# Moving a norm's centring and row scaling from VectorE to ScalarE, and one weighing past a unit's scores, in a two-layer graph attention kernel

## The chip, the cores and the metric

The kernel runs on one core of a Trainium2 chip. The metric is device time in microseconds (us) of one execution; the figure for the kernel before is the median of 3 runs.

## What is computed

The input x holds 64 graphs of 256 nodes with 512 features, and adj holds a 256x256 mask for each graph. Two attention layers follow one another, all in float32. Cut to what matters:

```
h = max(layernorm(x), 0)                     # layer 0
x = x + attention(h, adj; Wq, Wk, Wv, Wo)    # 4 heads of 64, masked softmax
h = max(layernorm(x), 0)                     # layer 1
h = layernorm(h) * gamma + beta              #   inside the second attention
x = x + attention(h, adj or diagonal; w_qkv, w_out)   # 8 heads of 64
```

In layer 0 the kernel normalises h as (h - mean) * r with r = (var + eps)^-0.5, and takes the maximum with 0 after the transpose. In layer 1 two norms follow each other. Since the first one's scale is positive, max(x - mean, 0) is kept unscaled as h, its own mean and variance are taken, and one row scale r serves both: (h - mean of h) * r.

## The kernel before

The work is cut into 32 steps of two graphs each (T = 512 tokens, four tiles of 128 rows, indexed t = 0 to 3). Each step goes through layer 0 and then layer 1. The heads are handled in pairs ("units"): layer 0 has two, layer 1 has four, written (layer, pair).

For each unit the path is: `project_qk` (L316) makes queries and keys; `scores` (L380) multiplies them, then VectorE adds the mask and takes a row minimum (L399), ScalarE takes the exponential with a row sum (L405), VectorE inverts the sum (L410), and the scaling by it is shared by VectorE (L415, one head of the pair) and ScalarE (L417, the other); `turn` (L420) transposes the result on TensorE, evicted by VectorE (L430) and ScalarE (L432), again one head each; `weigh` (L434) multiplies with the values and ScalarE copies the result out (L450). `combine` (L357) is the output projection, added to the residual by `accumulate` (L286). All projections are done by a fast matrix scheme with seven products on 2x2 blocks, numbered 1, 6, 7, 5, 2, 4, 3 in the order in which they are issued; their blocks need sums, which GpSimd forms (`act_sums`, L94). Products 2, 4 and 3 continue in the PSUM bank of 1, 7 and 5, so product 4 waits for the eviction of 7 (L276), and product 3 for that of 5 (L278).

The norms: `moments` (L196) takes the statistics of a row tile on VectorE (L198, L199). `norm0` (L213) does so for layer 0. `norm1` (L225) takes the statistics of x, centres and clips into h on VectorE (L233), and takes the statistics of h. When the last tile is through, `rsqrt` (L201) lets GpSimd raise the variance to -0.5 (L203), and `scale_row` (L206) subtracts the mean and multiplies by r on VectorE, in place (L208), once for each tile. `transpose_h` (L248) then transposes h on TensorE (L255), and ScalarE (layer 0, L259) or VectorE (layer 1, L261) evicts it.

What sets the order: each call is entered with a period and a place in it by `at` (L463); the calls are sorted by that time and traced in this order. On TensorE the traced order is the queue (L59). On the other engines the planner of the compiler orders instructions by when it expects them to be ready, with the traced order as priority; the result is a fixed queue for each engine. One period of steady work holds layer 1 of step s beside layer 0 of steps s+1 and s+2. Around place 3.0 of a period, TensorE's order is: the last products of `project_qk` for (1,1) and (1,3), `scores` (1,1) at 3.0, `combine` n=1 of layer 0 (entered at 9.0, that is place 3.0 of the period after its own), `weigh` (1,2) at 3.001, two transposes of layer 0, `combine` n=6, two more transposes, and the other products of the combination. Then follow norm1 from place 3.5 on, beside the projection of layer 0's queries and keys, `scores` (1,3) at 3.75, `turn` (1,3) at 4.25 and `weigh` (1,3) at 4.499; the row scaling of that norm is entered at 4.5.

[...] four in the pool "sc" (scores and turns) and four in the pool "mm" (everything else). The tile h has one buffer for both layers.

Of the kernel before, what the change touches and what calls it, by code (L numbers as in the profile page):

```python
# [8 lines left out]
FP = mybir.dt.float32  # L9
U8 = mybir.dt.uint8  # L10
AF = mybir.ActivationFunctionType
ALU = mybir.AluOpType
# [7 lines left out]
def kernel(  # L20
# [16 lines left out]
    nc = tc.nc  # L37
    P = 128
# [5 lines left out]
    NT = G * NIC  # L44
# [11 lines left out]
    stat = ctx.enter_context(tc.tile_pool(name="stat", bufs=4))  # L56
# [13 lines left out]
    mhalf = const.tile([P, NT], FP, name="mhalf")  # L70
# [96 lines left out]
    S = [dict() for _ in range(NSTEP)]  # L167
# [28 lines left out]
    def moments(mv, src, t):  # L196
        bs = stat.tile([P, 6], FP, name="bs")
        nc.vector.bn_stats(bs, src[:, t, :])  # L198
        nc.vector.bn_aggr(mv[:, t, :], bs)  # L199

    def rsqrt(var, name):  # L201
        r = stat.tile([P, NT], FP, name=name, bufs=2)
        nc.gpsimd.tensor_tensor(r, var, mhalf, ALU.pow)  # L203
        return r

    def scale_row(s, t):  # L206
        h, mean, r = S[s]["h"], S[s]["mean"], S[s]["r"]
        nc.vector.tensor_scalar(  # L208
            h[:, t, :], h[:, t, :], mean[:, t, 0:1], r[:, t:t + 1],
            op0=ALU.subtract, op1=ALU.mult,  # L210
        )

    def norm0(s, t):  # L213
        st = S[s]
        if t == 0:
            st["mean"] = stat.tile([P, NT, 2], FP, name="mv0", bufs=2)
        moments(st["mean"], st["h"], t)
        if t == NT - 1:
            ve = stat.tile([P, NT], FP, name="ve0", bufs=2)
            nc.vector.tensor_scalar(ve, st["mean"][:, :, 1], EPS, None, op0=ALU.add)  # L220
            st["r"] = rsqrt(ve, "r0")

    def norm1(s, t):  # L225
        st, x1 = S[s], S[s]["xt"]
        if t == 0:
            st["mv"] = stat.tile([P, NT, 2], FP, name="mv1", bufs=2)
            st["mean"] = stat.tile([P, NT, 2], FP, name="mg", bufs=2)
            st["h"] = act.tile([P, NT, D], FP, name="h")  # L230
        mv, mg, h = st["mv"], st["mean"], st["h"]
        moments(mv, x1, t)
        nc.vector.tensor_scalar(  # L233
            h[:, t, :], x1[:, t, :], mv[:, t, 0:1], 0.0, op0=ALU.subtract, op1=ALU.max
        )
        moments(mg, h, t)
        nc.gpsimd.tensor_tensor(x1[:, t, :], x1[:, t, :], bout_b, ALU.add)
        if t == NT - 1:
            ve = stat.tile([P, NT], FP, name="ve1", bufs=2)
            nc.vector.tensor_scalar(ve, mv[:, :, 1], EPS, EPS, op0=ALU.add, op1=ALU.mult)  # L240
            nc.vector.tensor_tensor(ve, ve, mg[:, :, 1], ALU.add)
            st["r"] = rsqrt(ve, "r1")


    def blocks_of(b, pairs):
# [217 lines left out]
    def at(period, place, fn, *args):  # L463
        events.append((period * PERIOD + place * SET, len(events), fn, args))

    def at_set(period, place, share, fn, *args):
        for i, n in enumerate((1, 6, 7, 5, 2, 4, 3)):
            at(period, place + i * share / 7, fn, *args, n)

    for s in range(NSTEP):  # L470

        p = s - 2
        at(p - 1, 5.6, load_h, s)
        for t in range(NT):
            at(p, 0.4 + 0.4 * t, norm0, s, t)
            at(p, 2.05 + 0.2 * t, scale_row, s, t)
        at(p, 2.9, mask, s, 0)
        for c in range(NC):
            at(p, 3.03 + 0.03 * c, transpose_h, s, 0, c)
        at_set(p, 3.5, 1.0, project_qk, s, 0, 0)  # L480
        at_set(p, 4.5, 0.5, project_v, s, 0)
        at(p, 4.5, scores, s, 0, 0)
        at(p, 5.15, turn, s, 0, 0)
        at(p, 5.6, scores, s, 0, 1)
        at(p, 5.601, weigh, s, 0, 0, True, False)
        at(p, 6.3, turn, s, 0, 1)
        at(p, 7.001, weigh, s, 0, 1, False, True)
        at(p, 7.4, load_x, s)
        at(p, 8.6, first_bias, s)
        at_set(p, 9.0, 0.5, combine, s, 0)  # L490
        for t in range(NT):
            at(p, 9.5 + 0.25 * t, norm1, s, t)
            at(p, 10.5 + 0.1 * t, scale_row, s, t)

        p = s
        for c in range(NC):
            at(p, -0.85 + 0.15 * c, transpose_h, s, 1, c)
        at(p, 0.3, mask, s, 1)
        at_set(p, 0.0, 1.0, project_qk, s, 1, 0)
        at_set(p, 1.0, 1.0, project_v, s, 1)  # L500
        at_set(p, 2.0, 1.0, project_qk, s, 1, 1)
        at(p, 1.0, scores, s, 1, 0)
        at(p, 1.65, turn, s, 1, 0)
        at(p, 2.0, scores, s, 1, 2)
        at(p, 2.001, weigh, s, 1, 0, True, False)
        at(p, 2.65, turn, s, 1, 2)
        at(p, 3.0, scores, s, 1, 1)
        at(p, 3.001, weigh, s, 1, 2, False, False)
        at(p, 3.5, turn, s, 1, 1)
        at(p, 3.75, scores, s, 1, 3)  # L510
        at(p, 3.751, weigh, s, 1, 1, False, False)
        at(p, 4.25, turn, s, 1, 3)
        at(p, 4.499, weigh, s, 1, 3, False, True)
        at_set(p, 5.0, 1.0, combine, s, 1)
        at(p, 6.0, store, s)
# [39 lines left out]
```

## Time and profile before

| | us |
|---|---|
| median of 3 runs | 3907.93 (3907.41 to 3910.31) |
| the profiled execution | 3909.91 |
| its span | 3908.1 |
| TensorE matmul busy | 3641.9 (93%) |
| VectorE busy | 2554.6 (65%) |
| ScalarE busy | 1683.9 (43%) |
| GpSimd busy | 1381.0 (35%) |

In the profile PE is TensorE's matmul, PEld its weight load, DVE is VectorE, ACT is ScalarE and POOL is GpSimd. A group of instructions is named by its line, its engine, and the program's names of its output and inputs (mm<-hT,wqkv). An entry "<- DVE qk L276" says which instruction ended a wait. In a timeline a row has a start, a duration, the engine, the line, the operation and a count; a bracket at its end is the idle time ahead of it. The granted TensorE clock was 0.986 of full speed over the span.

### The profile page before, as it was taken

Reading aid. Unit: us, or ns where it says so; the run is one execution under the profiler, and the core shown is the slowest. Engines: PE = TensorE matmul, PEld = TensorE weight load, DVE = VectorE, ACT = ScalarE, POOL = GpSimd, SP = SyncE. Lnnn points to the kernel's source line nnn. Section 1 sums busy time; section 2 is a strip of 40 time slices with the busy share of each in tenths; the row PEclk is TensorE's granted clock in tenths of the full one; section 3 lists DMA queues with packets and bytes.
Section 4 is the critical chain, followed back from the end, with each engine's and each line's share of the span. In section 5 each row is a group of like instructions: output and inputs, shape, how many; then the busy total and the mean of one; then the engine's idle time right before and its main releaser. Section 6 shows DMA issues by size and latency. Waiting matters only on the chain.

```text
span 3908.1 us, 58947 instructions
## 1 busy us (share of the span) xinstructions
PE 3641.9 (93%) x21953; PEld 3015.8 (77%) x21953; DVE 2554.6 (65%) x7193; ACT 1683.9 (43%) x4945; POOL 1381.0 (35%) x1170
## 2 busy tenths in 40 slices
PE   5999999999999999999999999999999999999988
PEld 4787778777777877788777878777887778787777
DVE  5666666676666666666766666666667666667664
ACT  2434444444444344444444443444444444434443
POOL 4243333343332433333433324333334333243331
PEclk8999999999999999999999999999999999999999
DMA  3011010110000110101100101101011001010000
GB/s 119 12 34 34 2 34 33 34 35 13 24 34 33 35 35 2 35 33 34 35 13 24 35 33 35 35 2 34 33 35 34 13 24 34 33 34 33 1 22 22
DMA packets 74127, 115.45 MB, mean 30 GB/s; under 512 B 18792, under 2 KB 22384, under 8 KB 73840
## 3 DMA queue, kind: packets, MB, share of 16 engines
q1 hardware_dynamic: 67584, 104.87, 8.1%
q10 hardware_dynamic: 6256, 6.82, 0.6%
q8 instruction: 172, 2.82, 0.3%
q14 instruction: 115, 0.94, 0.1%
HBM read 78.12 MB, written 33.55 MB: 29 GB/s over the span
## 4 chain that ended last, share of the span: by engine, by line
PE 69%; DVE 18%; ACT 9%; issue 2%; POOL 2%; DMA 1%; ACTq 0%; DVEq 0%; POOLq 0%
PE mm L328 20%; PE mm L365 14%; PE mm L350 13%; ACT pm L405 7%; PE sc L389 7%; PE mm L444 6%; PE sc L426 6%; DVE bs L198 3%; DVE pm L415 3%; DVE h L233 3%; PE mm L255 2%; DVE h L208 2%; DVE pm L399 1%; ACT pm L417 1%; DVE pm L430 1%
## 5 line engine op out<-in xcount | busy, mean ns | idle before, releaser
L328 PE MATMUL mm<-hT,wqkv 128*128 128x256 f32 x5376 | 1221.5, 382 | 55.7 <-DVE qk L276 43.5
L328 PEld LDWEIGHTS mm<-hT,wqkv 128*128 128x128 f32 x5376 | 1007.3, 191 | 221.8 <-issue 82.2
L405 ACT ACTIVATE pm<-pm,sa 128x256 f32<-128x256 f32 x1536 | 758.6, 495 | 589.5 <-DVE sa L399 589.5
L365 PE MATMUL mm<-wo,oT 128*128 128x256 f32 x2688 | 654.8, 393 | 92.1 <-ACT oT L450 72.1
L399 DVE CUSTOM_DVE_ANT_0 pm<-sc,n 128x256 f32<-128x256 f32 x1536 | 553.5, 417 | 242.3 <-PE sc L389 239.7
L350 PE MATMUL mm<-wqkv,hT 128*128 128x128 f32 (+1 forms) x3584 | 631.0, 331 | 17.9 <-DVE v L276 17.9
L365 PEld LDWEIGHTS mm<-wo,oT 128*128 128x128 f32 x2688 | 502.6, 195 | 185.7 <-issue 89.7
L350 PEld LDWEIGHTS mm<-wqkv,hT 128*128 128x128 f32 x3584 | 542.8, 191 | 101.6 <-issue 34.7
L294 POOL TENSOR_TENSOR xt<-xt,u 128x512 f32<-128x512 f32 x64 | 81.4, 1272 | 1304.5 <-DVE u L293 1304.5
L432 ACT COPY pm<-sc 128x512 f32<-128x512 f32 x384 | 225.1, 586 | 486.8 <-PE sc L426 486.7
L444 PE MATMUL mm<-pm,v 128*64 128x256 f32 x3072 | 377.3, 388 | 61.6 <-DVE pm L430 61.6
L417 ACT ACTIVATE pm<-pm,sa 128x256 f32<-128x256 f32 x768 | 345.3, 497 | 113.1 <-DVE sa L410 113.1
L389 PE MATMUL sc<-qk 64*128 64x256 f32 x3072 | 384.0, 389 | 0.7 <-DVE qk L284 0.7
L426 PE MATMUL sc<-ident,pm 128*128 128x128 f32 x3072 | 370.5, 274 | 8.8 <-DVE pm L415 8.7
L426 PEld LDWEIGHTS sc<-ident,pm 128*128 128x128 f32 x3072 | 347.8, 142 | 27.7 <-DVE pm L415 10.9
L444 PEld LDWEIGHTS mm<-pm,v 128*64 128x64 f32 x3072 | 205.0, 137 | 211.7 <-DVE pm L430 73.7
L415 DVE TENSOR_SCALAR pm<-pm,sa 128x256 f32<-128x256 f32 x768 | 355.8, 504 | 4.6
L389 PEld LDWEIGHTS sc<-qk 64*128 64x128 f32 x3072 | 278.6, 186 | 80.3 <-issue 47.1
L430 DVE COPY pm<-sc 128x512 f32<-128x512 f32 x384 | 252.6, 684 | 108.5 <-PE sc L426 108.4
L405 ACT ACTIVATION_READ_ACCUMULATOR pm<-pm,sa 128x1 f32 x1536 | 286.7, 187 | 0.0
L184 POOL TENSOR_TENSOR xt<-xt,bo_b 128x512 f32<-128x512 f32 x128 | 161.5, 1294 | 261.5 <-DMA xt<-in_x_dram 261.5
L96 POOL TENSOR_TENSOR oT<-oT 128x512 f32<-128x512 f32 (+1 forms) x64 | 68.9, 1077 | 379.0 <-ACT oT L450 379.0
(78 smaller groups left out, 3453.3 us busy)
## 6 DMA issues: line engine op xcount, KB each, us to landing
h<-in_x_dram SPq DMA_DIRECT2D x32, 1024.0 KB, 5.2
xt<-in_x_dram SPq DMA_DIRECT2D x32, 1024.0 KB, 5.2
out_dram<-xt SPq DMA_DIRECT2D x32, 1024.0 KB, 4.3
ad<-in_adj_dram SPq DMA_DIRECT2D x32, 128.0 KB, 2.2
wr<-in_L_gnn_w_qkv_dram ACTq DMA_DIRECT2D x3, 1024.0 KB, 8.9
wr<-in_L_gnn_w_out_dram ACTq DMA_DIRECT2D x1, 1024.0 KB, 9.4
wqkv<-in_L_gnn_Wq_dram ACTq DMA_DIRECT2D x4, 128.0 KB, 5.2
wqkv<-in_L_gnn_Wk_dram ACTq DMA_DIRECT2D x4, 128.0 KB, 4.0
```

The costliest lines, as they stand in the source:

```text
L328: nc.tensor.matmul(bank[:, k, :], w[:, wa, c, k, a * P:(a + 1) * P], st["hT"][:, ba, c, :], start=first and (k, c) == (0, 0), stop=(k, c) ...
L350: nc.tensor.matmul(bank[:, t, :], st["hT"][:, ba, c, t * P:(t + 1) * P], w[:, wa, c, 2, :], start=first and (t, c) == (0, 0), stop=(t, c) ...
L365: nc.tensor.matmul(bank[:, t, :], st[f"oT{lyr}"][:, ba, c, t * P:(t + 1) * P], w[:, wa, c, :], start=first and (t, c) == (0, 0), stop=(t, ...
L389: nc.tensor.matmul(sc[g, e][:, ic, :], qk[rows, 0, i0:i0 + P], qk[rows, 1, g * N:(g + 1) * N], start=True, stop=True,)
L399: nc.vector.tensor_tensor_reduce(out=pm[g, e][:, ic, :], in0=sc[g, e][:, ic, :], in1=neg[:, g * NIC + ic, :], scale=-SCALE, scalar=SMAX, o ...
L405: nc.scalar.activation(pm[g, e][:, ic, :], pm[g, e][:, ic, :], AF.Exp, bias=sa[:, 0, g, e, ic:ic + 1], scale=-1.0, accum_out=sa[:, 1, g, e ...
L415: nc.vector.tensor_scalar(pv, pv, inv, None, op0=ALU.mult)
L417: nc.scalar.activation(pv, pv, AF.Copy, scale=inv)
L426: nc.tensor.transpose(pp[:, jc, ic * P:(ic + 1) * P], pm[:, ic, jc * P:(jc + 1) * P], ident)
L430: nc.vector.tensor_copy(pm, pp)
L432: nc.scalar.copy(pm, pp)
L444: nc.tensor.matmul(po[e * DH:(e + 1) * DH, g, :], st[f"v{lyr}"][:, g * NIC + jc, c0:c0 + DH], pT[g, e][:, jc, :], start=(jc == 0), stop=(j ...
```

## The change

Three things change. First, `norm1` no longer centres and clips on VectorE: VectorE negates the mean into a third column of the statistics tile, and ScalarE computes Relu(x - mean) with this column as its bias. Second, `rsqrt` becomes `row_scales`: GpSimd computes r as before, then VectorE multiplies it by the negated mean to give mr, and `scale_row` runs on ScalarE as Identity with scale r and bias mr, in both layers. The tiles r and mr have three buffers each, shared by the two layers. Third, `weigh` of unit (1,2) is entered at place 2.999 in place of 3.001, which puts it ahead of `scores` (1,1) and of `combine` n=1 of layer 0 on TensorE.

```diff
--- before.py
+++ after.py
@@ -196,18 +196,23 @@
     def moments(mv, src, t):
         bs = stat.tile([P, 6], FP, name="bs")
         nc.vector.bn_stats(bs, src[:, t, :])
-        nc.vector.bn_aggr(mv[:, t, :], bs)
-
-    def rsqrt(var, name):
-        r = stat.tile([P, NT], FP, name=name, bufs=2)
-        nc.gpsimd.tensor_tensor(r, var, mhalf, ALU.pow)
-        return r
+        nc.vector.bn_aggr(mv[:, t, 0:2], bs)
+
+    def row_scales(s, var):
+
+        st = S[s]
+        st["r"] = stat.tile([P, NT], FP, name="r", bufs=3)
+        st["mr"] = stat.tile([P, NT], FP, name="mr", bufs=3)
+        nc.gpsimd.tensor_tensor(st["r"], var, mhalf, ALU.pow)
+        nc.vector.scalar_tensor_tensor(
+            st["mr"], st["mean"][:, :, 0], -1.0, st["r"], op0=ALU.mult, op1=ALU.mult
+        )
 
     def scale_row(s, t):
-        h, mean, r = S[s]["h"], S[s]["mean"], S[s]["r"]
-        nc.vector.tensor_scalar(
-            h[:, t, :], h[:, t, :], mean[:, t, 0:1], r[:, t:t + 1],
-            op0=ALU.subtract, op1=ALU.mult,
+        h = S[s]["h"]
+        nc.scalar.activation(
+            h[:, t, :], h[:, t, :], AF.Identity,
+            bias=S[s]["mr"][:, t:t + 1], scale=S[s]["r"][:, t:t + 1],
         )
 
     def norm0(s, t):
@@ -218,28 +223,27 @@
         if t == NT - 1:
             ve = stat.tile([P, NT], FP, name="ve0", bufs=2)
             nc.vector.tensor_scalar(ve, st["mean"][:, :, 1], EPS, None, op0=ALU.add)
-            st["r"] = rsqrt(ve, "r0")
+            row_scales(s, ve)
 
 
 
     def norm1(s, t):
         st, x1 = S[s], S[s]["xt"]
         if t == 0:
-            st["mv"] = stat.tile([P, NT, 2], FP, name="mv1", bufs=2)
+            st["mv"] = stat.tile([P, NT, 3], FP, name="mv1", bufs=2)
             st["mean"] = stat.tile([P, NT, 2], FP, name="mg", bufs=2)
             st["h"] = act.tile([P, NT, D], FP, name="h")
         mv, mg, h = st["mv"], st["mean"], st["h"]
         moments(mv, x1, t)
-        nc.vector.tensor_scalar(
-            h[:, t, :], x1[:, t, :], mv[:, t, 0:1], 0.0, op0=ALU.subtract, op1=ALU.max
-        )
+        nc.vector.tensor_scalar(mv[:, t, 2:3], mv[:, t, 0:1], -1.0, None, op0=ALU.mult)
+        nc.scalar.activation(h[:, t, :], x1[:, t, :], AF.Relu, bias=mv[:, t, 2:3])
         moments(mg, h, t)
         nc.gpsimd.tensor_tensor(x1[:, t, :], x1[:, t, :], bout_b, ALU.add)
         if t == NT - 1:
             ve = stat.tile([P, NT], FP, name="ve1", bufs=2)
             nc.vector.tensor_scalar(ve, mv[:, :, 1], EPS, EPS, op0=ALU.add, op1=ALU.mult)
             nc.vector.tensor_tensor(ve, ve, mg[:, :, 1], ALU.add)
-            st["r"] = rsqrt(ve, "r1")
+            row_scales(s, ve)
 
 
     def blocks_of(b, pairs):
@@ -505,7 +509,7 @@
         at(p, 2.001, weigh, s, 1, 0, True, False)
         at(p, 2.65, turn, s, 1, 2)
         at(p, 3.0, scores, s, 1, 1)
-        at(p, 3.001, weigh, s, 1, 2, False, False)
+        at(p, 2.999, weigh, s, 1, 2, False, False)
         at(p, 3.5, turn, s, 1, 1)
         at(p, 3.75, scores, s, 1, 3)
         at(p, 3.751, weigh, s, 1, 1, False, False)
```

## The prediction

> **What bounds the kernel now.** I read the page first, then who waited for whom on TensorE, then the chain of waits through one steady period, then the timelines of ScalarE and TensorE where it leaves TensorE. The page's first section (engine, busy us, share of the span, instructions):
>
> ```profile
> PE 3641.9 (93%) x21953; PEld 3015.8 (77%) x21953; DVE 2554.6 (65%) x7193; ACT 1683.9 (43%) x4945; POOL 1381.0 (35%) x1170
> ```
>
> TensorE is the bound: 266 us of 3908.1 is all that it idles, so more than that can't be won by taking work off other engines. The table of waits of TensorE says where it idles (total, times, longest):
>
> ```profile
> PE mm L365 <- ACT oT L450: 72.1, 30, 2.4
> PE mm L444 <- DVE pm L430: 61.6, 30, 2.1
> PE mm L328 <- DVE qk L276: 43.5, 30, 1.7
> PE mm L255 <- DVE h L208: 21.7, 3, 17.6
> PE mm L350 <- DVE v L276: 17.9, 30, 0.9
> ```
>
> Four waits recur 30 times, once in each steady period (about 120 us: h is loaded at 1920.95 and again at 2040.72); L208's is the start-up. The chain of waits, from 1999.32, shows that two of the four are one stretch of VectorE work (start, us, what; the middle cut):
>
> ```profile
> 1999.32 1.11 PE sc L389 x8
> 2000.44 0.03 issue
> 2000.46 0.67 DVE qk L274
> 2001.14 0.09 DVE mg L199
> 2001.22 0.58 DVE bs L198
> 2001.80 0.32 DVE pm L399
> ...
> 2006.20 1.39 DVE h L233
> ...
> 2010.75 0.49 DVE h L233
> ...
> 2014.03 1.91 DVE h L208 x4
> 2015.94 0.60 DVE qk L282
> 2016.54 0.61 DVE pm L430
> 2017.15 0.04 issue
> 2017.19 1.95 PE mm L444 x16
> ```
>
> From 2000.44 to 2017.19 the end is set by the second norm on VectorE, interleaved with the softmax of scores(1,3); TensorE loses 1.20 us (L276) and 2.05 us (L430) in it, 3.25 together. The last lines show the mechanism: four row scalings and L282 stand on VectorE's queue ahead of L430, the eviction that the weighing needs. The fourth (L350, 0.6 each) lies behind and the change doesn't touch it.
>
> The L365 wait is another place. TensorE and, below it, ScalarE:
>
> ```profile
> 2097.59 2.00 PE L389 MATMUL sc<-qk 64*128 64x256 f32 x16
> 2100.58 1.95 PE L444 MATMUL mm<-pm,v 128*64 128x256 f32 x16
> 2102.46 1.09 PE L255 MATMUL mm<-ident,h 128*128 128x128 f32 x8
> 2105.96 2.05 PE L365 MATMUL mm<-wo,oT 128*128 128x256 f32 x4 [2.41 <-ACT oT L450]
> 2107.80 1.63 PE L255 MATMUL mm<-ident,h 128*128 128x128 f32 x8
> ```
> ```profile
> 2104.44 0.91 ACT L417 ACTIVATE pm<-pm,sa 128x256 f32<-128x256 f32 x2
> 2105.24 0.57 ACT L450 COPY oT<-mm 128x512 f32<-128x512 f32 x1
> ```
>
> The weighing ends at 2102.5; its copy L450 stands behind the whole softmax on ScalarE, until 2105.8, and so keeps one of the four PSUM banks "mm". Combine n=1 holds one, two transposes the others; combine n=6 finds none.
>
> [...] The page of before has one table load (1283 ns) with Exp, Copy and Relu in use, so Identity should bring none. [...] L233 goes from 486 to 1377 ns, the longest beside L188 and L192 on GpSimd; L208 has a median of 541.
>
> **Part 1, centring and scaling on ScalarE.** Removed from VectorE: L233, 128 x 902 ns = 115 us, and L208, 256 x 550 = 125 (62.9 + 62.3 in the rows). Added to it: 128 negations of 128x1 and 64 products of 128x4, none of which the trace has; nearest are L220 (170) and L410 (174), so 192 x 0.17 = 33 us, between 0.10 and 0.26 (L240) each. VectorE ends near 2347. [...] Totals bind nowhere; the places do.
>
> *Layer 0's norm* (scaling near 2053) lies beside 10 us without a wait: its transposes come at 2102, and the two L432 that could queue behind 2.9 us of scaling feed a weighing at 2065.6. Cost nothing; uncovered it would be 2.9 us a period.
>
> *The second norm* is the stretch above. On its chain:
> - Ahead of the first L399 VectorE loses two L233 (0.49 + 1.07 in its timeline) and gains two negations (0.3): the delay of 1.36 before 2001.80 shrinks by about 1.2.
> - L233 of rows 2 and 3: 1.88 off, two negations 0.3 on, and w, VectorE's new waits: L198 of h now follows ScalarE. Queued behind that L198 are L278, L240, L241; for these wait GpSimd's r and TensorE. A Relu takes 0.7 and the next row's L198 (0.68) covers it, so w is about 0.4 for handovers; from 0 (ScalarE sits idle 1.54 before L417 at 2009.01) to 3.1, if each Relu stands behind two exponentials (0.98) and L450 (0.56): 2 x (0.98 + 0.56 + 0.71 - 0.68).
> - The end: off go L208 x4, L282 and L430 (1.91 + 0.60 + 0.61 = 3.12). But ScalarE has the other half of that turn's evictions, L432. On VectorE the planner put all four scalings ahead of L282 and L430, thus took r for early; I take it that ScalarE's queue gets the same order. Then on the path are the product with r (0.25 with handovers), four scalings (4 x 0.71 + 0.09 = 2.92) and one L432 (0.59): 3.76, 0.64 more than before.
>
> Sum: -1.2 - 1.88 + 0.3 + w + 0.64 = w - 2.14; with w = 0.4, 1.74 us less a period, of the 3.25 there are.
>
> GpSimd: L237 now follows the Relu of its row, but that comes earlier than L233 did; nothing.
>
> *Start-up*: L255 waits until 22.67 because L208 is interleaved with weight sums on VectorE. ScalarE is free from 15.7; four scalings end near 18.6: up to 4 us. Later GpSimd's weight sums hold TensorE for 12.2 us anyway, so I take 3, from 0 to 5.
>
> **Part 2, the weighing ahead of the scores.** No instruction is added; it is moved past 16 score matmuls on TensorE, and its L450 past the softmax on ScalarE; it issues no DMA and no GpSimd sums there. Its inputs, L430 and L432, end at 2094.5 and 2094.9; it would start at 2097.6: 2.7 us of cover, nothing lost. L450 then runs near 2099.6 on an idle ScalarE, and the wait of n=6 (2.41) goes. What is late next: the scores start 1.88 later, so do exponentials and L417, which end at 2105.35 + 1.88 = 2107.23 with L259, the copy of the first transpose, behind them. TensorE reaches n=6 at 2103.6, then needs a bank for the third transpose: L259's, free at about 2107.75, or that of n=6, whose L293 needs L291 (about 2106.4) and ends at 2107.1. Before, the third transpose started at 2107.80. So of 2.41 only 0 to 0.95 is kept; I take 0.5.
>
> **The sum.** (1.74 + 0.5) x 30 = 67, start-up 3: 70 us. The profiled execution took 3909.9 (span 3908.1), less 70 is 3840; it lies 2 above the median of the runs, so 3838.
>
> **Rivals.**
> - B, L432 goes ahead of the scalings and no Relu is waited for: both stalls go (61.6 + 43.5 = 105), 0.9 x 30 = 27 from the banks, 3 at the start: 3773. For it: L432 precedes the scalings in program order; ScalarE idles around. Against: the order of L208 before L282.
> - C, w is about 1.6 and the bank keeps 0.2: (0.54 + 0.2) x 30 + 3 = 25: 3883. For it: exponentials fill ScalarE from 2002.2 to 2006.9.
> - D, slower: ScalarE's queue puts the Relus of rows 2 and 3 behind exponentials and L450, VectorE stands at L198, and the L432 stand behind the scalings; w = 3.1, the bank keeps nothing: 0.96 x 30 = 29 more, less 3 at the start: 3934. It decides from w = 2.14 + 0.5 = 2.6 on. Against: the 1.54 us of idle ScalarE right there.
> - E, the stretch is held by other waits and the bank by L259: within 0.2%, 3906.
>
> **Chances.** My forecast 0.48, B 0.20, C 0.13, D 0.16, E 0.03. A difference under 0.2% (8 us) is about what can't be told from no change. Faster 0.80 (one hundredth of C counts as the same), same 0.04, slower 0.16. The range takes in B and C and leaves D out: 3772 to 3900.
>
> **What would show it.** Right: L450's wait at L365 gone, and a wait of L255 on L259 or L293 of 1.5 to 2.4 us in its place; L444's wait on L430 replaced by one on ACT L432 of about 1.5; L276's 43.5 mostly gone; VectorE near 2347, ScalarE near 1943. Wrong: waits of VectorE's L198 on ACT's h of over 2 us a period (D), no wait at L444 at all (B), a second table load.

## The result and the profile after

The changed kernel took 3909.64 us (median; 3909.23 to 3912.22) beside 3908.09 for the kernel before (median of four runs on the same chip): a ratio of 1.0004, 95% interval 0.9987 to 1.0022. No difference can be measured. The forecast was 3838, with a range of 3772 to 3900: it was wrong. The number of case E, to which I had given 0.03, is the one that came out, but not its reason: the bank was not held by L259, and the stretch of the second norm did become shorter, as will be seen. The profiled execution took 3909.23 with a span of 3907.4.

The lines used below stand 4 to 6 lower in the changed kernel: L365 is now L369, L450 is L454, L444 is L448, L255 is L259, L328 is L332, L350 is L354, L276 is L280, L293 is L297, L430 is L434, L432 is L436, L208 is L213, L233 is L239.

The first section of the page of the changed kernel (engine, busy us, share, instructions) shows that the work moved as planned:

```profile
PE 3656.7 (94%) x21953; PEld 3044.9 (78%) x21953; DVE 2410.3 (62%) x7001; ACT 1940.0 (50%) x5329; POOL 1379.9 (35%) x1170
```

VectorE lost 144 us and ScalarE gained 256. But TensorE, with the same 21953 matmuls, is busy 14.8 us longer, which no instruction of the change explains. Its table of waits (total, times, longest), to be held against the five lines of before:

```profile
PE mm L259 <- DVE u L297: 95.7, 30, 3.2
PE mm L354 <- DVE v L280: 58.3, 31, 1.9
PE mm L448 <- DVE pm L434: 28.3, 30, 1.0
PE mm L259 <- ACT h L213: 21.4, 8, 18.2
```

Of the old waits, the one for L276 at the queries and keys (43.5 us) vanished, and the one at the weighing fell from 61.6 to 28.3. But the combination's wait of 2.4 us came back as one of 3.2 at the third transpose, and the wait at the values (L354) grew from 0.6 a period to 1.9. Two new or larger waits took the place of those removed.

**The first place.** TensorE of the changed kernel around the weighing that was moved (start, us, engine, line, operation, count; the bracket is the idle time ahead):

```profile
1973.02 1.95 PE L448 MATMUL mm<-pm,v 128*64 128x256 f32 x16
1974.90 2.00 PE L393 MATMUL sc<-qk 64*128 64x256 f32 x16
1976.82 1.13 PE L369 MATMUL mm<-wo,oT 128*128 128x256 f32 x4
1977.79 1.04 PE L259 MATMUL mm<-ident,h 128*128 128x128 f32 x8
1978.66 1.03 PE L369 MATMUL mm<-wo,oT 128*128 128x256 f32 x4
1982.88 1.97 PE L259 MATMUL mm<-ident,h 128*128 128x128 f32 x8 [3.19 <-DVE u L297]
```

The weighing (first row) runs ahead of the scores, and the combination's second product (fifth row) no longer waits: that much is as forecast. The third transpose, last row, now takes the stall. It needs a PSUM bank again: L297 on VectorE empties one, and L297 needs L295, a copy on ScalarE. ScalarE of the same stretch:

```profile
1981.28 0.56 ACT L295 COPY u<-mm 128x512 f32<-128x512 f32 x1
1981.74 0.91 ACT L421 ACTIVATE pm<-pm,sa 128x256 f32<-128x256 f32 x2
```

L295 stands inside the softmax of `scores` (1,1), which now starts 1.9 us later because the weighing went first. The third transpose starts 9.86 us after the weighing's start; the prediction had 9.5 to 10.2. The start of this transpose was read rightly; what it is worth was not, as shown below.

**The second place.** ScalarE of the changed kernel, around the second norm:

```profile
2008.12 1.05 ACT L436 COPY pm<-sc 128x512 f32<-128x512 f32 x2
2012.19 2.93 ACT L213 ACTIVATE h<-h,mr,r 128x512 f32<-128x512 f32 x4 [3.02 <-DVE mr L207]
...
2015.75 0.51 ACT L409 ACTIVATE pm<-pm,sa 128x256 f32<-128x256 f32 x1
```

The evictions L436 went ahead of the four row scalings. The prediction had them behind. Instead it is the next unit's work that stands behind the scalings: ScalarE waits 3.02 us for mr, then scales for 2.93, and only at 2015.75 does the exponential of the next layer-0 scores begin. VectorE shows what that delays:

```profile
2014.31 0.42 DVE L403 CUSTOM_DVE_ANT_0 pm<-sc,n 128x256 f32<-128x256 f32 x1 [1.56 <-PE sc L393]
2017.87 0.18 DVE L414 RECIPROCAL sa<-sa 128x4 f32<-128x4 f32 x1 [1.05 <-ACT pm L409]
2018.28 1.63 DVE L419 TENSOR_SCALAR pm<-pm,sa 128x256 f32<-128x256 f32 x2
2020.34 0.42 DVE L280 TENSOR_TENSOR v<-mm,v 128x256 f32<-128x256 f32 x1
```

L414 and L419 wait for the exponentials, and L280, which TensorE needs for the values, stands behind them until 2020.8. That is the 1.9 us at L354.

**The third thing** is no wait. The clock record has stretches of 3.41 us in which the clock granted to TensorE is 0.50 of full speed; such a stretch is called a drop below. Stretches of the changed kernel around the 3.19 us stall (stretch and length, then PE, PEld, DVE, ACT, POOL busy with counts, the granted clock, DMA share, GB/s):

```profile
1978.85:1982.26 3.41, 0.84 (x4) 0.39 (x3) 1.64 (x8) 3.41 (x13) 0.00 (x0) 1.00 0.00 0
1982.26:1985.67 3.41, 2.79 (x11) 2.61 (x12) 0.57 (x1) 2.54 (x5) 2.61 (x3) 0.50 0.00 0
```

In the first stretch TensorE is busy 0.84 us of 3.41; in the next it has half the clock (0.50). The same view of the kernel before, in a period with such a drop and in one without:

```profile
1982.70:1986.11 3.41, 1.08 (x10) 0.84 (x8) 0.79 (x3) 3.41 (x11) 0.00 (x0) 1.00 0.00 0
1986.11:1989.52 3.41, 3.33 (x12) 2.90 (x13) 0.69 (x1) 1.30 (x3) 0.41 (x1) 0.50 0.00 0
...
1863.23:1866.64 3.41, 1.73 (x16) 1.04 (x12) 1.33 (x7) 3.41 (x11) 0.00 (x0) 1.00 0.00 0
1866.64:1870.05 3.41, 2.68 (x15) 2.29 (x16) 0.69 (x1) 2.64 (x6) 0.70 (x1) 1.00 0.00 0
```

The wait is the same 2.40 us in both periods of before. In the steady parts of both executions the drops start on one grid of 3.413 us, and the stretches shown are cut on it. Where one of them held most of the wait (1.08 busy), the next was granted half the clock; where the wait straddled two of them (1.73 busy), it was not. Over the whole execution the clock record of before has 27 half-speed stretches (111 us in all, some of several grid lengths in the start-up and at the end), with one in about two of three steady periods; that of after has 43 (169 us), at least one in every period and in some two. What they cost can be read from the same two periods of before, from one load of h to the next, in the same columns:

```profile
1802.14:1920.95 118.81, 112.14 (x686) 92.94 (x686) 79.26 (x225) 52.37 (x154) 42.67 (x36) 1.00 0.09 28
1920.95:2040.72 119.77, 113.54 (x686) 94.25 (x686) 78.90 (x225) 52.47 (x154) 42.68 (x36) 0.99 0.09 28
```

The same 686 matmuls take 1.40 us more with a drop. The period grows by only 0.96, because the wait for L276 behind it shrinks from 1.6 to 1.2.

### The profile page after: what moved, and what is told of

Its sections match the earlier page's. It is cut to its first block, busy times and chain, and to the rows that moved or that the text cites. A ratio compares the mean times of both kernels' runs of the same rounds, so it can differ in the third digit from the quotient of the medians.

```text
span 3907.4 us, 59075 instructions
## 1 busy us (share of the span) xinstructions
PE 3656.7 (94%) x21953; PEld 3044.9 (78%) x21953; DVE 2410.3 (62%) x7001; ACT 1940.0 (50%) x5329; POOL 1379.9 (35%) x1170
## 5 line engine op out<-in xcount | busy, mean ns | idle before, releaser
L332 PE MATMUL mm<-hT,wqkv 128*128 128x256 f32 x5376 | 1214.0, 381 | 10.8 <-POOL hT L98 10.3
L332 PEld LDWEIGHTS mm<-hT,wqkv 128*128 128x128 f32 x5376 | 1009.2, 191 | 167.5 <-issue 24.6
L354 PE MATMUL mm<-wqkv,hT 128*128 128x128 f32 (+1 forms) x3584 | 639.0, 334 | 58.3 <-DVE v L280 58.3
L369 PE MATMUL mm<-wo,oT 128*128 128x256 f32 x2688 | 667.9, 399 | 19.4 <-POOL oT L98 17.9
L354 PEld LDWEIGHTS mm<-wqkv,hT 128*128 128x128 f32 x3584 | 550.3, 194 | 141.8 <-DVE v L280 64.2
L369 PEld LDWEIGHTS mm<-wo,oT 128*128 128x128 f32 x2688 | 521.5, 202 | 111.0 <-POOL oT L98 19.0
L419 DVE TENSOR_SCALAR pm<-pm,sa 128x256 f32<-128x256 f32 x768 | 415.4, 582 | 5.7
L448 PE MATMUL mm<-pm,v 128*64 128x256 f32 x3072 | 374.8, 386 | 28.3 <-DVE pm L434 28.3
L436 ACT COPY pm<-sc 128x512 f32<-128x512 f32 x384 | 217.9, 583 | 328.4 <-PE sc L430 328.3
L430 PE MATMUL sc<-ident,pm 128*128 128x128 f32 x3072 | 370.8, 274 | 8.9 <-DVE pm L419 8.7
L430 PEld LDWEIGHTS sc<-ident,pm 128*128 128x128 f32 x3072 | 347.9, 142 | 27.9 <-DVE pm L419 11.1
L448 PEld LDWEIGHTS mm<-pm,v 128*64 128x64 f32 x3072 | 203.9, 137 | 177.1 <-issue 43.8
L434 DVE COPY pm<-sc 128x512 f32<-128x512 f32 x384 | 254.3, 682 | 108.9 <-PE sc L430 108.8
L213 ACT ACTIVATE h<-h,mr,r 128x512 f32<-128x512 f32 x256 | 191.1, 805 | 204.7 <-DVE mr L207 204.7
L259 PE MATMUL mm<-ident,h 128*128 128x128 f32 x1024 | 166.1, 301 | 117.1 <-DVE u L297 95.7
```

The costliest lines, as they stand in the source:

```text
L332: nc.tensor.matmul(bank[:, k, :], w[:, wa, c, k, a * P:(a + 1) * P], st["hT"][:, ba, c, :], start=first and (k, c) == (0, 0), stop=(k, c) ...
L354: nc.tensor.matmul(bank[:, t, :], st["hT"][:, ba, c, t * P:(t + 1) * P], w[:, wa, c, 2, :], start=first and (t, c) == (0, 0), stop=(t, c) ...
L369: nc.tensor.matmul(bank[:, t, :], st[f"oT{lyr}"][:, ba, c, t * P:(t + 1) * P], w[:, wa, c, :], start=first and (t, c) == (0, 0), stop=(t, ...
L419: nc.vector.tensor_scalar(pv, pv, inv, None, op0=ALU.mult)
L430: nc.tensor.transpose(pp[:, jc, ic * P:(ic + 1) * P], pm[:, ic, jc * P:(jc + 1) * P], ident)
L434: nc.vector.tensor_copy(pm, pp)
```

## Experiments

Two theories stood against each other. "Waits": the time follows from the plain waits of the path, so each edit's gain or loss adds up. "Clock", in its strict form: the drops pin the mean period to whole windows of the clock (35 x 3.413 = 119.47 us, which is what both kernels show), so no small edit moves it. For each run I read the mean of the steady periods and the length of a period whose clock record has no drop; what lies between is, but for a few hundredths of a us, the cost of drops. Both are from the profiled execution; the time is the median of the runs.

| kernel | period without a drop, us | mean | drops' part | time |
|---|---|---|---|---|
| before | 118.83 | 119.48 | 0.65 | 3908.1 |
| after | 117.54 (from e6) | 119.46 | 1.92 | 3909.6 |
| e1, part 1 alone | 117.16 | 117.99 | 0.83 | 3864.5 |
| e2, part 2 alone | none seen | 120.33 | | 3939.1 |
| e3, before, TensorE longer | 119.26 | 120.11 | 0.85 | 3921.9 |
| e4, after, TensorE longer | none seen | 119.47 | | 3912.8 |
| e5, after, first wait filled | 117.54 | 118.94 | 1.40 | 3893.1 |
| e6, after, both waits filled | 117.54 | 117.54 | no drop | 3856.7 |
| e7, before, wait filled | 118.83 | 119.50 | 0.67 | 3906.9 |
| e8, after, early order | 115.92 | 115.95 | no drop | 3803.9 |
| e9, before, early order | 116.81 | 117.35 | 0.54 | 3852.3 |
| e10, e1, a scaling on VectorE | 116.77 | 117.31 | 0.54 | 3839.9 |
| e12, e8, a scaling on VectorE | 115.34 | 115.34 | no drop | 3783.9 |
| e13, e8, half that scaling | 115.75 | 115.75 | no drop | 3795.7 |

**e1: part 1 without part 2.** The changed kernel with the weighing put back.

```diff
-        at(p, 2.999, weigh, s, 1, 2, False, False)
+        at(p, 3.001, weigh, s, 1, 2, False, False)
```

> Part 1 alone: both norms on ScalarE, the weighing of unit (1,2) where it was. Theory 'clock': the mean period of the steady part is held at 35 windows of 3.413 us = 119.47 us by TensorE's clock, which drops to half for one window after a window in which TensorE idled much; what the waits lose or gain inside a period is made up by more or fewer such drops. It expects no change, 3908 within 4 us. Theory 'waits': the change came out even because part 1 wins and part 2 loses in plain waiting time; by the segments of the two profiles part 1 is worth -1.70 - 1.10 + 1.53 = -1.27 us a period, so 3870.

3864.51 us, ratio 0.9886 (0.9873 to 0.99). Part 1 alone wins 1.1%, which the strict clock theory excluded. A period without a drop is 1.67 us shorter than before. Its waits:

```profile
PE mm L369 <- ACT oT L454: 72.1, 30, 2.4
PE mm L354 <- DVE v L280: 58.2, 31, 1.9
PE mm L448 <- DVE pm L434: 28.4, 30, 1.0
```

The combination's wait is that of before, the other two those of after: each part owns its waits.

**e2: part 2 without part 1.** The kernel before with the one line of the weighing changed from 3.001 to 2.999.

> Part 2 alone: the weighing ahead of the scores, the norms on VectorE. Theory 'clock': no change, 3908 within 4 us. Theory 'waits': the segments around the combination are 0.05 + 1.22 = 1.27 us a period longer in the changed kernel, so 3946.

3939.08 us, ratio 1.0076 (1.0063 to 1.0088): slower by 0.8%, between the two figures expected. Its waits have the bank's 3.2 us in place of 2.4; the one at the weighing is as before, the one for L276 fell from 43.5 to 27.0:

```profile
PE mm L255 <- DVE u L293: 95.7, 30, 3.2
PE mm L444 <- DVE pm L430: 61.7, 30, 2.1
PE mm L328 <- DVE qk L276: 27.0, 30, 1.5
```

Every steady period has at least one drop, so this run doesn't tell how much of the loss is plain waiting. The two parts nearly cancel: part 1 wins 44 us alone, part 2 loses 31 alone and 45 on top of part 1 (3909.6 against 3864.5).

**e3 and e4: TensorE 0.4 us longer.** Four transposes of `turn` (1,0) are issued twice, in the kernel before (e3) and in the changed one (e4); the second issue is extra work with the same result.

```diff
+                    for _ in range(2 if (lyr, pr, g, e) == (1, 0, 0, 0) else 1):
                         nc.tensor.transpose(
```

> The kernel before, with four of the sixteen transposes of turn (1,0) issued twice: 0.44 us of TensorE work a step at a place without a wait, the queues of the other engines unchanged. Theory 'clock': the periods are 118.83 us without and 119.78 us with a drop, so anything up to 119.47 - 118.83 = 0.64 us that is added is absorbed by fewer drops... the mean stays at 119.47 as long as 118.83 + 0.44 = 119.27 is below it; no change, 3908 within 4 us. Theory 'waits': 32 x 0.44 = 14 us longer, 3922.

> The changed kernel with the same 0.44 us of TensorE work more a step. Theory 'clock': its periods are 119.21 us with one drop, 120.84 with two; with 0.44 more the second drop is no longer needed and the first one is left out at times; the mean stays at 119.47, 3910 within 4 us. Theory 'waits': 14 us longer, 3924.

e3: 3921.91, ratio 1.0036 (1.0023 to 1.0048), the plain sum of 'waits'. e4: 3912.79, ratio 1.0012 (1.0005 to 1.0018), where the plain sum was about 14 us more than the changed kernel and 3 came. In e4, 28 periods in a row are 119.47 us within 0.04, with the drop 66.8 us behind the load of h each time: there the period did lock to 35 windows, and the small extra work vanished in it. With e1 to e3 that strict form falls as a general rule. What is left is the weaker one: the time is the plain path plus what the drops cost.

**e5: the first wait of the changed kernel filled.** 24 transposes of the identity, into a bank that nobody reads, are put on TensorE ahead of the third transpose. They add work and save none.

```diff
+    def warm(n):
+        pw = ps_sc.tile([P, NIC, N], FP, name="sc")
+        for _ in range(n):
+            nc.tensor.transpose(pw[:, 0, :P], ident, ident)
...
+        at(p, 3.085, warm, 24)
```

> The changed kernel with 24 idle transposes of the identity (2.6 us at 0.109 each, into a free PSUM tile that nobody reads) issued on TensorE just ahead of the third transpose of layer 0, where it idles 3.19 us; from the start-up on the queues of the other engines are the same. Theory 'clock' (the half-speed window that follows this idle stretch in every period slows the products behind it): the stretch from the third transpose to turn (1,1) falls from 6.88 us to the 5.43 that it has in periods without a drop, 1.45 a period: 3866. Theory 'waits' (the clock adds nothing, the move of the weighing costs what the later copies cost): no change, 3909.

3893.13, ratio 0.9963 (0.9951 to 0.9976): between the two figures expected. The waits:

```profile
PE mm L354 <- DVE v L280: 58.4, 31, 1.9
...
PE mm L259 <- DVE u L297: 17.2, 30, 0.6
```

The stall is filled down to 0.6. But the drop moved to the next wait of that size, at the values, as TensorE's timeline shows:

```profile
1978.83 4.48 PE L369 MATMUL mm<-wo,oT 128*128 128x256 f32 x20
...
2014.49 2.73 PE L354 MATMUL mm<-wqkv,hT 128*128 128x128 f32 x16 [1.91 <-DVE v L280]
2017.02 4.65 PE L369 MATMUL mm<-wo,oT 128*128 128x256 f32 x16
```

The combination behind the filled wait runs 20 matmuls in 4.48 us; the one behind the values' wait needs 4.65 for 16. A period with such a drop is 119.20 us, one without 117.54: 1.66 us. In the changed kernel some periods have two drops; here none in the steady part has more than one, and four of 27 have none. So 24 matmuls a period that compute nothing won 16 us over the changed kernel.

**e7: the same in the kernel before**, with 18 transposes at its combination (`at(p, 3.065, warm, 18)`).

> The kernel before with 18 such transposes (2.0 us) ahead of combine n=6, where TensorE idles 2.41 us. Theory 'clock': every period becomes one without a drop, 118.83 in place of 119.47 us, 30 x 0.64 = 19 less: 3889. Theory 'waits': no change, 3908.

3906.86, ratio 0.9996 (0.9988 to 1.0005): nothing won. The drop moved here too, to the weighing's wait for L430:

```profile
2014.38 3.63 PE L444 MATMUL mm<-pm,v 128*64 128x256 f32 x16 [2.06 <-DVE pm L430]
```

At full clock these 16 matmuls took 1.95 us behind the same wait (before, 1897.42). A single filler can't tell the theories apart as long as another wait of 1.9 us or more follows.

**e6: both waits of the changed kernel filled**, e5 with 16 more transposes at the values:

```diff
+        at(p, 4.85, warm, 16)
```

> The changed kernel with idle transposes in both long waits of TensorE: 24 ahead of the third transpose of layer 0 (wait 3.19 us) and 16 ahead of the sixth product of layer 0's values (wait 1.91 us). With the first alone the half-speed window moved to the second wait, and periods with it took 119.2, those without 117.54. Theory 'clock': no wait is left that is long enough, every period takes 117.54; 3909 - 30 x (119.46 - 117.54) = 3851. If the drop moves on to the remaining wait of 0.94 us at weighing (1,3), or the gain of the first run had another cause: 3893 again.

3856.68, ratio 0.9869 (0.9855 to 0.9882). Not one drop is left in the steady part and every period there is 117.52 to 117.56 us. The waits:

```profile
PE mm L448 <- DVE pm L434: 28.3, 30, 1.0
PE mm L259 <- DVE u L297: 17.2, 30, 0.6
PE mm L354 <- DVE v L280: 5.0, 30, 0.2
```

The remaining 1.0 us sets off no drop. Forty matmuls a period that compute nothing win 53 us over the changed kernel. This settles that the drops, and not a hidden wait, hold the changed kernel at 119.46.

**e8 and e9: the bank's wait taken away.** The first product of the combination and the layer-0 transposes are entered ahead of the scores and its softmax, in the changed kernel (e8) and in one with both norms on VectorE as before, but with the weighing moved (e9).

```diff
-            at(p, 3.03 + 0.03 * c, transpose_h, s, 0, c)
+            at(p, 2.9 + 0.02 * c, transpose_h, s, 0, c)
...
-        at_set(p, 9.0, 0.5, combine, s, 0)
+        at(p, 8.9995, combine, s, 0, 1)
+        for i, n in enumerate((6, 7, 5, 2, 4, 3)):
+            at(p, 9.0 + (i + 1) * 0.5 / 7, combine, s, 0, n)
```

> The changed kernel with the four transposes of layer 0 and its combine n=1 ahead of the weighing and the scores too, so that ScalarE's copies of all of them come ahead of the softmax. Both theories: the wait of the third transpose (3.19 us) goes. By plain waiting the stretch from the end of turn (1,2) to turn (1,1) falls from 20.29 us to the 15.2 of TensorE's own work, 5.1 a period (of which 'clock' puts 1.45 down to the half-speed window): 3909 - 153 = 3756; if copies of the combination hold TensorE at its second product instead, some 1.5 of this stays: 3801.

> The norms on VectorE as before, with the order of the best run so far: the four transposes of layer 0, the weighing and combine n=1 ahead of the scores. If plain waits and clock drops add up as found, this takes the wait at the combination away (115.93 us a period with the norms on ScalarE, where no period has a drop), and the norms on VectorE cost their 118.83 - 117.16 = 1.67 us: 117.6 a period, and with a drop in one period of two at the waits of 2.05 us that are left another 0.6: 3853 to 3871. If the norms cost nothing where no drop is: 3804.

e8: 3803.88, ratio 0.9734 (0.972 to 0.9747), close to the smaller of the two gains expected (3801), though not for the reason given there: the bank's wait is gone and no copy of the combination holds TensorE for long, but a wait for L280 at the queries and keys came up.

```profile
PE mm L332 <- DVE qk L280: 48.6, 30, 1.9
PE mm L354 <- DVE v L280: 43.2, 31, 1.7
```

e9: 3852.32, ratio 0.9856 (0.9843 to 0.987), just under the 3853 to 3871 expected, but with other parts: a period without a drop takes 116.81 where 117.6 was expected. So the early order is worth 1.4% without part 1, and part 1 another 48 us on top of it (3803.9 against 3852.3): 0.89 us a period in plain waiting and 0.54 in drops, of which e8 has none.

**e10: the second norm's scaling back on VectorE**, in e1; layer 0's stays on ScalarE. The new branch of `scale_row` (the calls for the second norm select it):

```diff
...
+            nc.vector.tensor_scalar(
+                h[:, t, :], h[:, t, :], S[s]["r"][:, t:t + 1], S[s]["mr"][:, t:t + 1],
+                op0=ALU.mult, op1=ALU.add,
+            )
...
```

> Part 1 alone, but with the row scaling of the second norm on VectorE as before (as h times r plus mr); the centring and layer 0's scaling stay on ScalarE. It tells what the four scalings ahead of the exponentials on ScalarE cost. If they are what holds VectorE's v L280 (1.91 us in place of 0.58), the stretch from weighing (1,3) to the combination falls from 12.6 to 11.2 us; the scalings return to VectorE ahead of L430 and turn (1,3) to weighing (1,3) rises from 4.59 by up to 1.1. So between 3864 - 40 = 3824 (no new wait) and 3860 (both cancel). If the exponentials are late for another reason: 3864 + 33 = 3897.

3839.85, ratio 0.9826 (0.9812 to 0.9839), 25 us less than e1. In its table of waits (lines 6 lower again) the values' 58.2 us are down to 9.8, which shows that the scalings on ScalarE had caused them, and a part came back in another:

```profile
PE mm L375 <- ACT oT L460: 72.0, 30, 2.4
PE sc L399 <- DVE qk L294: 29.1, 30, 1.0
...
PE mm L360 <- DVE v L286: 9.8, 31, 1.6
```

**e12 and e13: the edits that won, together.** e12 is e8 with the second norm's scaling on VectorE as in e10; e13 gives VectorE only every second row (`t % 2 == 1`).

> The early order with the norms on ScalarE but the second norm's row scaling on VectorE. Alone that scaling on VectorE was worth 117.16 - 116.77 = 0.39 us a period in periods without a drop. No drop is left in the early order, so: 115.93 - 0.39 = 115.54, 3804 - 12 = 3792. If the two gains overlap: 3804.

> As the last one, with two of the second norm's four rows scaled on VectorE and two on ScalarE. If what counts is when the last row leaves ScalarE's queue, then half the delay of the exponentials goes and the evictions on VectorE wait for two scalings only: better than both, 3780 to 3790. If the planner interleaves them worse: 3804.

e12: 3783.93, ratio 0.9683 (0.967 to 0.9696), faster than forecast and faster than both kernels by 3.2%. e13: 3795.71, ratio 0.9712 (0.9699 to 0.9725), 12 us more than e12 and neither of the two figures expected: halving the row scalings between the engines gives no extra. e12's page and its largest waits (lines again 6 lower):

```profile
PE 3617.1 (96%) x21953; PEld 3000.0 (79%) x21953; DVE 2460.7 (65%) x7129; ACT 1858.9 (49%) x5201; POOL 1384.5 (37%) x1170
```

```profile
PE mm L338 <- DVE qk L286: 48.4, 30, 1.6
PE mm L360 <- DVE v L286: 25.8, 31, 2.1
```

With the same 21953 matmuls TensorE is busy 39.6 us less than in the changed kernel: only 7 half-speed stretches (40 us) are left in its clock record, all of them in the start-up or behind the last load of h.

## Why the prediction was wrong, point by point

**Part 1: right, for reasons that were half wrong.** The costs of single instructions came out as taken. The groups of the changed kernel (busy us and mean ns of one, then the idle time before):

```profile
L213 ACT ACTIVATE h<-h,mr,r 128x512 f32<-128x512 f32 x256 | 191.1, 805 | 204.7 <-DVE mr L207 204.7
L239 ACT ACTIVATE h<-xt,mv 128x512 f32<-128x512 f32 x128 | 92.4, 722 | 153.1 <-DVE mv L238 153.1
L238 DVE TENSOR_SCALAR mv<-mv 128x1 f32<-128x1 f32 x128 | 19.6, 153 | 4.3
```

What Relu and Identity of this form would cost was my estimate, which no trace of before shows. A Relu was taken at 0.7 us and took 722 ns; four scalings in a row were taken at 2.92 us and took 2.93 (at 2012.19; they overlap, as 4 x 805 ns would be 3.22). The negation and product were taken at 170 and took 153 and 163 to 179. ScalarE was to end near 1943 and came to 1940.0, with one table load (1283 ns, as in before). VectorE was to end near 2347 and came to 2410: L419 grew from a mean of 504 to 582 ns. Two readings in the prediction were loose and did no harm: 256 x 550 ns is 141 us, and 125 is what L208 kept VectorE busy, since its instructions overlap (four in a row took 1.91 us, with a median of 541 ns for one); and the 31 longest L233 (1258 to 1377 ns) lie beside L192 alone, not L188, while the 35 with nothing on GpSimd beside them took 486 to 489.

A period was to be 1.74 us shorter; e1 measured 1.67. But the split was another. From the scores (1,3) to the weighing it was more, 2.8 to 3.0 us, since L436 went ahead of the scalings, which is what rival B said (VectorE did wait for a Relu there, 0.71 us in the period shown above, where w was taken as 0.4); and 1.3 came back at L280, behind those scalings, which no case of mine had. That 1.67 is so near to 1.74 is luck: two errors of over 1 us each cancelled.

**Part 2: the first step that failed, the baseline.** "Before, the third transpose started at 2107.80. So of 2.41 only 0 to 0.95 is kept; I take 0.5." The new time of the third transpose was right. The baseline was not. The period whose timeline I had read, around 2105, was one with a clock drop: its row of the combination behind the wait is 2.05 us for four matmuls. In a period without one it is

```profile
1867.37 1.10 PE L365 MATMUL mm<-wo,oT 128*128 128x256 f32 x4 [2.40 <-ACT oT L450]
```

From the end of `turn` (1,2) to the third transpose, before takes 13.76 us with a drop but 12.84 without; after takes 13.41. Against the first there is a gain of 0.35, against the second a loss of 0.57. From there to `turn` (1,1) it is 5.43 before and 5.25 after without drops, so the plain loss is 0.4 a period (117.16 in e1 to 117.54). I forecast a gain of 0.5, so this step is worth 26 us of the miss.

**The second step that failed, and the larger: the clock was put at nothing.** The page showed a granted clock of 0.986, the timeline showed a row twice as long as its like, and the prediction used neither. Part 2 made the longest recurring stall 3.19 us in place of 2.41, and then every steady period had a drop; part 1 took away the wait for L276, which before had swallowed 0.44 us of each drop (a drop at the combination costs 0.96 in before and 1.42 in e1, where that wait is gone). The cost of drops rose from 0.65 to 1.92 us a period, which is 38 us of the miss.

**The sum with what was measured.** Against the forecast of 3840 for the profiled execution: part 1 is 0.07 a period short, part 2 is 0.88 the other way (0.5 gained, 0.38 lost), the drops cost 1.27 more. Over 30 periods: 2 + 26 + 38 = 66. The start-up gained 6.2 (I took 3, at most 5) and the stretch behind the last load of h took 5.3 more, which I had at nothing: another 2. Together 68, and 3909.2 - 3840 = 69.

**Of what was to be seen**: L450's wait is gone, as said, and one of the third transpose stands in its place, but 3.2 us long where 1.5 to 2.4 was given. The wait at the weighing stayed on VectorE (0.94) and did not go to ScalarE. The wait for L276 went, and that at the values, which "lies behind and the change doesn't touch it", trebled.

**What stays open.** A period of the changed kernel without drops was seen only in e5 and e6, with idle transposes in it, so part 2's plain loss of 0.38 rests on them. The changed kernel agrees with them: its periods with two drops take 120.85 us and those with one 119.21, 1.64 a drop, so one without any would take about 117.57 (an estimate). Of the 1.29 us by which periods without a drop became shorter, the tables of waits show 0.7 (6.7 us in a period of before, 6.0 after); the rest is in TensorE's modelled busy time and was not traced. Nor was the longer end behind the last load of h.

## What to carry to other kernels

Before a gain is read from a timeline, look at the clock granted there, and take the baseline from a period in which it was full. On this kernel, which TensorE bounds, stalls of 1.9 us and more were in many periods paid twice, once as the wait and once as a slower clock behind it (0.50 for 3.41 us), while those of 1.6 in e8 and e12 set off no drop; an edit that shortens other waits and lengthens the longest can win nothing. And when an engine's work is moved to a second one, follow what stands behind it in the second one's queue, also the work of another step: the row scalings held up none of the transposes of h that need them, and cost the values of layer 0 1.3 us.

## What the runs showed of the hardware

In these runs the clock granted to TensorE fell to 0.50 for a stretch of 3.41 us after a stretch of the same length that held little matmul work, and this cost up to 1.68 us (e1: periods of 118.84 and 117.16). The steady parts of all fourteen profiles (from 250 us to 350 us before the end), each cut on the grid of its own drops, show where the border lies. Of the stretches at full clock, those with less than 1.38 us of matmuls (158) were all followed by a drop, and those with more than 1.52 never; in between, some 50 were and some 30 were not. In before and after by themselves it is 34 of 34 below 1.38, none of 1826 above 1.52, and 16 of 24 in between. What decides there was not found. One of e5 (the first pair of lines) held 1.52 us and was followed by a drop; one of before (the second pair) held 1.42 and was not:

```profile
466.03:469.44 3.41, 1.52 (x13) 1.33 (x13) 3.17 (x8) 2.60 (x10) 2.54 (x2) 1.00 0.00 0
469.44:472.85 3.41, 3.41 (x14) 3.05 (x14) 0.97 (x3) 0.68 (x3) 0.00 (x0) 0.50 0.00 0
...
1893.95:1897.36 3.41, 1.42 (x7) 0.91 (x5) 3.10 (x7) 0.37 (x1) 0.27 (x1) 1.00 0.00 0
1897.36:1900.77 3.41, 3.35 (x28) 2.39 (x30) 1.20 (x3) 0.86 (x2) 0.69 (x1) 1.00 0.00 0
```

The ends of matmuls are modelled in the profile, which may blur this border. In the steady part of e6 the emptiest stretch has 2.45, in e8 and e12 it has about 1.8, and no drop comes. From 1030.38 to 3419.71 us the drops of before start on one grid of 3.4133 us within 0.003, and the clock records of before and after hold no rates but 1.00 and 0.50. Whether the border lies at the same place for other shapes of matmul was not tried.

With one wait filled, the drop went to another long wait (e5: 1.91 us, at the values; e7: 2.06, at the weighing). In e4 it held the loop at a whole number of these stretches: 28 periods took 119.47 us, 35 x 3.413, and the added work, which cost the kernel before 14 us, cost 3.
